# A conv, mixture-of-experts and Mamba-style block on one core: the second expert product with its weights stationary, and the image added during dispatch

## The chip, the cores and the metric

The kernel runs on one core of a Trainium2 chip. The time is the device time of one execution, in microseconds (us). A core has five engines that take their instructions in order, each from its own queue, and meet only through semaphores: TensorE (PE, the matmuls; its weight loads are shown apart as PEld), VectorE (DVE), ScalarE (ACT), GpSimd (POOL) and SyncE (SP, which here only issues DMA transfers). POOL also issues the indirect transfers, the scatters.

## The reference

The input x is 32 images of 128 channels by 56 x 56 points, float32; T = 32 x 3136 = 100352 tokens, C = 128. Two layers follow each other.

```python
# layer 0
x = depthwise_conv7x7(input) + dw_bias            # then NHWC
x = layernorm(x) * ln_gamma + ln_beta
logits = x.reshape(T, C) @ Wg + bg                # 8 experts
topv, topi = top_k(logits, 2); wts = softmax(topv)
# tokens in order of falling wts[:, 0]; an expert takes at most cap = 15680 rows
h = gelu(einsum('ecd,edf->ecf', eb, W1) + b1)     # 512 hidden channels
y = einsum('ecf,efd->ecd', h, W2) + b2
moe = sum over the two experts of y[slot] * gate
out0 = input + x + layer_scale * moe
# layer 1
xh = cv1 @ out0;  l = silu(batchnorm(dwconv3x3(xh)))
g = mamba(layernorm(xh))                          # a scan over 3136 points, 256 channels, 16 states
out = out0 + cv2 @ concat(l, g)
```

## The kernel before

The program has five stages, one after the other, with DRAM buffers between them.

*Convolution and layer norm* (lines 304 to 468). A depthwise convolution as banded matmuls, the norm, the router's logits. A normalized row is stored in `res_d`, one row of 128 floats for each token. Within two image rows (112 tokens, `TT`) the columns come out mirrored, so a row of `res_d` isn't in image order; `perm` is the 112 x 112 matrix that undoes this.

*Routing* (475 to 672). A counting loop finds for each expert the limit of its capacity, then every (token, choice) pair gets a slot: a row of `buf_d`, or a spare row behind the 8 x 15680 real ones where the expert is full. Beside it, 28 transfers write the real rows of `buf_d` with zeros and, in the last column, the token number T (lines 481 to 486). A row of `buf_d` has 130 words: 128 values, the gate, and the number of the row in `res_d` it goes back to.

*Dispatch* (834 to 865). 56 iterations. Each loads 14 x 128 rows of `res_d` into `xg` (line 853, six buffers), ACT copies them for the second choice (854), DVE writes the gates and the row numbers (856, 857; the numbers come from `backs`, made by an iota at 843), and POOL issues 28 scatters of 128 rows into `buf_d` (859). In the middle of it the weights of layer 1 are prepared.

*Experts* (871 to 957). For each of 8 experts, 31 groups of up to 512 rows (30 full ones and one of 320). A group is loaded as `xb` (945, ten buffers), transposed on PE into `ept` (951), copied by ACT to `xc` (953). `products` is called for the group before: four matmuls of 512 columns with a slice of W1 stationary and `xc` moving (890), each followed by a Gelu on ACT into `hh` (893); then for each of four tiles of 128 rows four matmuls with `hh` stationary and a slice of W2 moving (897), so that the result `py` has one row on one partition; DVE adds the bias (903), multiplies by the gate (906); POOL scatters 128 rows at a time and adds them to `res_d` (911), with a bounds check that leaves out rows with number T. In float32 each matmul is two instructions, a transpose is one. The order on each engine is made by a list scheduler from the program's order. The weights of an expert are loaded into one of two buffers (929 to 938): those of expert e + 2 as soon as expert e is done, and W2 and b2 are multiplied by the layer scale on DVE (935, 938).

*Layer 1* (960 to 1430). 224 groups of 448 points, 16 states each, in an order written out by hand (`PLAN`, `UNITS`): each step has a place in units of a state, and all are sorted by it. `fetch` (1011) loads 448 points of the input image (`x1`) and the rows of `res_d` (`yg`); `moe_pe` (1022) makes their sum in PSUM, with the image through the identity and the rows through `perm`, and `moe_act` (1032) copies it to `x1`, from which everything else follows. DVE scans the states (1373, 1377) and shares the products with POOL (1397); POOL makes `db` (1336), ACT the exponentials (1354), PE sums the products (1286).

Of the kernel before, what the change touches and what calls it, by code (L numbers as in the profile page):

```python
# [5 lines left out]
F32 = mybir.dt.float32  # L6
# [238 lines left out]
def tile_kernel(tc: tile.TileContext, a: dict, out: bass.AP):  # L245
# [14 lines left out]
    with (  # L260
# [6 lines left out]
        res_d = dram.tile([T, C], F32, name="res_d")  # L267

        ident = const.tile([128, 128], F32, name="ident")
        make_identity(nc, ident)  # L270
        mean_w = const.tile([128, 128], F32, name="mean_w")
# [203 lines left out]
        with (  # L475
# [5 lines left out]
            zero = rt.tile([128, ZT, RW], F32, name="zero")  # L481
            nc.gpsimd.memset(zero, 0.0)
            nc.gpsimd.memset(zero[:, :, C + 1].bitcast(I32), T)
            buf_t = buf_d[: E * CAP].rearrange("(p k) c -> p k c", p=128)
            for k in range(0, E * CAP // 128, ZT):
                nc.sync.dma_start(out=buf_t[:, k : k + ZT, :], in_=zero)
# [188 lines left out]
        def weights(wp, wt, pw):  # L675
# [86 lines left out]
            nc.tensor.matmul(p[:, 0:1], lhsT=mean_w, rhs=cv1b, start=True, stop=True)  # L762
# [71 lines left out]
        with (  # L834
# [3 lines left out]
            tc.tile_pool(name="disp", bufs=6, reuse_waits="tile") as dp,  # L838
        ):
            backs = []  # L840
            for k in range(2):
                bi = dc.tile([128, QB, TT], I32, name=f"bi{k}")
                nc.gpsimd.iota(bi, pattern=[[TT, QB], [1, TT]], base=0, channel_multiplier=PT)
                backs.append(bi)

            XT = 14
            res_b = res_d[:T, :].rearrange("(j q p) c -> q j p c", q=QB, p=TT)
            for q in range(QB):
                for p0 in range(0, TT, XT):
# [5 lines left out]
                    for k, xg in enumerate(xgs):  # L855
                        nc.vector.tensor_copy(xg[:, :, C], gates[k][:, o : o + XT])  # L856
                        nc.vector.tensor_copy(xg[:, :, C + 1].bitcast(I32), backs[k][:, q, ps])
                        for j in range(XT):
                            apart(nc.gpsimd.indirect_dma_start(  # L859
                                out=buf_d[:, :],  # L860
                                out_offset=bass.IndirectOffsetOnAxis(ap=slots[k][:, o + j : o + j + 1], axis=0),
                                in_=xg[:, j, :], in_offset=None,
                            ), "scatter")
                if q == QB // 2:
                    w3 = weights(w3p, w3t, p3t)
# [5 lines left out]
        with (  # L871
# [3 lines left out]
            tc.tile_pool(name="eph", bufs=3, space=PSUM) as eph,  # L875
            tc.tile_pool(name="epy", bufs=2, space=PSUM) as epy,
        ):
            lsr = ew.tile([128, C], F32, name="lsr", bufs=1)
            nc.sync.dma_start(
                out=lsr, in_=a["L0_conv_layer_scale"].rearrange("c a b -> (c a b)").partition_broadcast(128)  # L880
            )
            todo = []

            def products(e, tiles, xb, xc, w1t, w2t, b1t, b2t):

                rows = sum(tiles)
                hh = eb.tile([128, KF, GT * 128], F32, name="hh")
                for k in range(KF):
                    ph = eph.tile([128, GT * 128], F32, name="ph")
                    nc.tensor.matmul(  # L890
                        ph[:, :rows], lhsT=w1t[:, k * 128 : (k + 1) * 128], rhs=xc[:, :rows], start=True, stop=True
                    )
                    nc.scalar.activation(hh[:, k, :rows], ph[:, :rows], AF.Gelu, bias=b1t[:, k : k + 1])  # L893
                py = epy.tile([128, GT, C], F32, name="py")
                for j, n in enumerate(tiles):
                    for k in range(KF):
                        nc.tensor.matmul(  # L897
                            py[:n, j, :], lhsT=hh[:, k, j * 128 : j * 128 + n], rhs=w2t[:, k, :],
                            start=k == 0, stop=k == KF - 1,
                        )  # L900
                ys = eb.tile([128, GT, C], F32, name="ys", bufs=6)
                for j, m, n in wholes(tiles):
                    nc.vector.tensor_tensor(  # L903
                        ys[:n, j:m, :], py[:n, j:m, :], b2t[:n].unsqueeze(1).to_broadcast([n, m - j, C]), ALU.add
                    )
                    nc.vector.tensor_tensor(
                        ys[:n, j:m, :], ys[:n, j:m, :], xb[:n, j:m, C : C + 1].to_broadcast([n, m - j, C]), ALU.mult
                    )

                for j, n in enumerate(tiles):  # L910
                    apart(nc.gpsimd.indirect_dma_start(  # L911
                        out=res_d[:, :],
                        out_offset=bass.IndirectOffsetOnAxis(ap=xb[:n, j, C + 1 : C + 2].bitcast(I32), axis=0),
                        in_=ys[:n, j, :], in_offset=None, bounds_check=last, oob_is_err=False, compute_op=ALU.add,
                    ), f"back{e}")
# [11 lines left out]
            last = nc.gpsimd.to_reg(T - 1)  # L927
            for e in range(E):
# [7 lines left out]
                b2t = ew.tile([128, C], F32, name="b2t")  # L936
                nc.sync.dma_start(out=b2t, in_=a["L0_conv_b2"][e].partition_broadcast(128))
                nc.vector.tensor_tensor(b2t, b2t, lsr, ALU.mult)
                for i0 in range(0, CAP, GT * 128):
                    rows = min(GT * 128, CAP - i0)  # L940
                    tiles = [min(128, rows - j) for j in range(0, rows, 128)]
                    xb = eb.tile([128, GT, RW], F32, name="xb", bufs=10)
                    for j, m, n in wholes(tiles):
                        r0 = e * CAP + i0 + j * 128
                        nc.sync.dma_start(
                            out=xb[:n, j:m, :],
                            in_=buf_d[r0 : r0 + (m - j) * n, :].rearrange("(k p) c -> p k c", p=n),
                        )
                    pt = ept.tile([C, GT * 128], F32, name="ept")
                    for j, n in enumerate(tiles):  # L950
                        nc.tensor.transpose(pt[:, j * 128 : j * 128 + n], xb[:n, j, :C], ident[:n, :n])  # L951
                    xc = eb.tile([C, GT * 128], F32, name="xc")
                    nc.scalar.copy(xc[:, :rows], pt[:, :rows])
                    if todo:
                        products(*todo.pop())
                    todo.append((e, tiles, xb, xc, w1t, w2t, b1t, b2t))
            products(*todo.pop())


# [9 lines left out]
def layer1(s):  # L969
# [5 lines left out]
    mm_tile, res_d, x_d, out_d = s["mm_tile"], s["res_d"], s["x_d"], s["out_d"]  # L975
    perm = s["perm"]
# [5 lines left out]
    with (  # L982
# [28 lines left out]
        def fetch(g):  # L1011
# [3 lines left out]
            d["x1"] = three.tile([C, CH1], F32, name="x1", bufs=5)  # L1015
            nc.sync.dma_start(out=d["x1"], in_=x_d[n, :, q * CH1 : (q + 1) * CH1])
            d["yg"] = two.tile([TT, TPC1, C], F32, name="yg")
            nc.sync.dma_start(
                out=d["yg"], in_=res_d[t0 : t0 + CH1, :].rearrange("(j p) c -> p j c", p=TT)
            )  # L1020

        def moe_pe(g):
# [3 lines left out]
            nc.tensor.matmul(p[:, :CH1], lhsT=ident, rhs=d["x1"], start=True, stop=False)  # L1026
            for j in range(TPC1):
                nc.tensor.matmul(
# [3 lines left out]
        def moe_act(g):  # L1032
            d = st[g]
            nc.scalar.copy(d["x1"], d.pop("p_moe")[:, :CH1])
# [431 lines left out]
```

## Time and profile before

| | us |
|---|---|
| median of 14 runs | 15843.06 (15838.17 to 15858.88) |
| the profiled execution | 15853.05 |
| its span, first to last instruction | 15851.3 |
| convolution and norm, up to the last store of `res_d` | 0 to 1535 |
| routing, up to the first load of the dispatch | 1773 |
| dispatch, first scatter to last | 1779 to 3944 |
| experts, first load of `xb` to last scatter | 3946 to 5886 |
| layer 1, from the first load of `yg` | 5888 to 15851 |

All lines of a profile are in microseconds, unless marked ns. A line of the groups gives the line of the program, the engine, the operation, the tile written and the tiles read, the shapes, how often it ran, then the busy time and the mean of one in ns, then the idle time of the engine just before such instructions and what ended most of it. A line of the timeline gives the start, the duration, the engine, the line, the operation, the tiles, the shapes and the count, and in brackets the idle time before it and its releaser. "issue" means that nothing the profile shows was waited for. Matmuls overlap in their pipeline, so a matmul's own duration is longer than the distance to the next one. The two groups of scatters and the largest of layer 1 are:

```profile
L1336 POOL TENSOR_TENSOR db<-du,bb 128x1792 f32<-128x1792 f32 x1792 | 6579.1, 3683 | 0.1
L1373 DVE TENSOR_TENSOR_SCAN da<-da,db 128x898 f32<-128x898 f32 x2240 | 4521.8, 2019 | 0.6 <-issue 0.5
L859 POOL DMA_INDIRECT buf_d<-xg,slot x1568 | 1643.7, 1048 | 525.5 <-issue 521.0
L911 POOL DMA_INDIRECT res_d<-ys,xb x984 | 1592.6, 1619 | 349.2 <-issue 282.7
```

### The profile page before, as it was taken

What the parts mean: (1) busy time and instruction counts of PE and PEld (TensorE: products, weight loads), DVE (VectorE), ACT (ScalarE), POOL (GpSimd) and SP (SyncE); (2) the same over time, 40 slices, a digit from 0 to 9 for tenths busy, and PEclk for the clock granted to TensorE, in tenths of its full rate; (3) what the DMA queues carried; (4) which work ended last, traced back from release to release, by engine and by line L of the source; (5) the groups of instructions that cost most, each with busy time, mean ns of one, the idle gap of its engine ahead of it and who ended that gap; (6) DMA issues with size and microseconds to landing.
All of it is one profiled execution on the core that took longest, in us unless ns stands there. A gap on an engine that the chain in (4) does not pass through costs nothing. (4 is left out here: it accounts for less than half of the span.)

```text
span 15851.3 us, 247520 instructions
## 1 busy us (share of the span) xinstructions
PE 12825.1 (81%) x92981; PEld 7168.3 (45%) x92981; DVE 11114.2 (70%) x11366; ACT 10495.6 (66%) x21038; POOL 13327.5 (84%) x6330
## 2 busy tenths in 40 slices
PE   7996200000999999999999999999999999999998
PEld 7996100000777764444444444444444444444444
DVE  2655400000111119999999999999999999999999
ACT  4564300000444448888888888888888888888888
POOL 2343377777888879999999999999999999999999
PEclk9997555555999999999999999999999999999999
DMA  8785422222555545555555555555555555555555
GB/s 262 230 235 172 178 72 71 71 71 62 70 72 70 72 64 184 184 184 185 184 184 184 185 185 183 184 183 184 184 185 184 184 184 185 185 184 184 183 184 170
DMA packets 1325280, 2520.85 MB, mean 159 GB/s; under 512 B 139352, under 2 KB 777136, under 8 KB 1316400
## 3 DMA queue, kind: packets, MB, share of 16 engines
q1 hardware_dynamic: 1127600, 2310.57, 45.5%
q0 software_dynamic: 196480, 194.45, 7.0%
q8 instruction: 732, 11.99, 0.3%
q14 instruction: 468, 3.83, 0.1%
HBM read 2129.06 MB, written 375.43 MB: 158 GB/s over the span
## 5 line engine op out<-in xcount | busy, mean ns | idle before, releaser
L1336 POOL TENSOR_TENSOR db<-du,bb 128x1792 f32<-128x1792 f32 x1792 | 6579.1, 3683 | 0.1
L1354 ACT ACTIVATE da<-dt,aneg 128x449 f32<-128x449 f32 x7168 | 4540.2, 637 | 375.8 <-DVE r L1095 112.9
L1373 DVE TENSOR_TENSOR_SCAN da<-da,db 128x898 f32<-128x898 f32 x2240 | 4521.8, 2019 | 0.6 <-issue 0.5
L1286 PE MATMUL py<-prod,ident 64*64 64x448 f32 x28672 | 3225.9, 547 | 120.3 <-DVE prod L1397 112.8
L1397 POOL TENSOR_TENSOR prod<-hs,cb 128x896 f32<-128x896 f32 x1344 | 2605.0, 1938 | 219.4 <-issue 160.6
L1397 DVE TENSOR_TENSOR prod<-da,cb 128x896 f32<-128x896 f32 x2240 | 2439.0, 1089 | 132.4 <-DMA cb<-bc_d 17.1
L859 POOL DMA_INDIRECT buf_d<-xg,slot x1568 | 1643.7, 1048 | 525.5 <-issue 521.0
L911 POOL DMA_INDIRECT res_d<-ys,xb x984 | 1592.6, 1619 | 349.2 <-issue 282.7
L951 PE MATMUL ept<-ident,xb 128*128 128x128 f32 (+1 forms) x984 | 189.0, 274 | 2078.8 <-DMA xb<-buf_d 2078.2
L1373 DVE TENSOR_TENSOR_SCAN hs<-da,db 128x898 f32<-128x898 f32 x896 | 1785.2, 2013 | 0.1
L1286 PEld LDWEIGHTS py<-prod,ident 64*64 64x64 f32 x28672 | 1007.6, 132 | 1558.9 <-issue 1068.9
L1126 PE MATMUL p_xm<-te,wk 128*128 128x448 f32 x3584 | 1395.5, 540 | 0.0
L903 DVE TENSOR_TENSOR ys<-py,b2t 128x512 f32<-128x512 f32 (+2 forms) x256 | 170.8, 670 | 1729.5 <-PE py L897 1618.0
L856 DVE COPY xg<-gate 128x14 f32<-128x14 f32 x112 | 20.4, 185 | 1883.9 <-DMA buf_d<-xg,slot 1847.7
L854 ACT COPY xg<-xg 128x1792 f32<-128x1792 f32 x56 | 94.5, 1688 | 1821.5 <-DMA buf_d<-xg,slot 1773.2
L951 PEld LDWEIGHTS ept<-ident,xb 128*128 128x128 f32 (+1 forms) x984 | 124.6, 143 | 2082.5 <-issue 2081.3
L897 PEld LDWEIGHTS py<-w2t,hh 128*128 128x128 f32 x7872 | 938.0, 191 | 191.6 <-issue 119.4
L897 PE MATMUL py<-w2t,hh 128*128 128x128 f32 x7872 | 987.5, 279 | 14.8 <-ACT hh L893 9.4
L1126 PEld LDWEIGHTS p_xm<-te,wk 128*128 128x128 f32 x3584 | 671.6, 189 | 665.3 <-issue 567.5
L379 PE MATMUL pc<-xc,toep 112*112 112x112 f32 (+1 forms) x8192 | 939.1, 270 | 36.5 <-ACT toep L368 32.5
L1377 DVE TENSOR_TENSOR_SCAN hs<-da,db 128x449 f32<-128x449 f32 x896 | 925.0, 1075 | 0.5 <-ACT da L1354 0.3
L1258 PE MATMUL p_l<-xh,dwd 64*64 64x224 f32 x16128 | 907.1, 352 | 21.9 <-ACT dt L1240 2.2
(241 smaller groups left out, 20279.9 us busy)
## 6 DMA issues: line engine op xcount, KB each, us to landing
bb<-bc_d SPq DMA_DIRECT2D x1792, 448.0 KB
cb<-bc_d SPq DMA_DIRECT2D x1792, 448.0 KB
toep<-toep_d SPq DMA_DIRECT2D x448, 392.0 KB
buf_d<-zero SPq DMA_DIRECT2D x28, 2275.0 KB
xb<-buf_d SPq DMA_DIRECT2D x240, 260.0 KB
xt<-in_x SPq DMA_DIRECT2D x32, 1568.0 KB
res_d<-xa SPq DMA_DIRECT2D x128, 392.0 KB
xg<-res_d SPq DMA_DIRECT2D x56, 896.0 KB
```

The source lines that it names most:

```text
L379: nc.tensor.matmul(pc[:, c, :, lo:hi], lhsT=tp[c // 2][:, c % 2, 6 - 2 * o : 8 - 2 * o, :], rhs=s4[:, c, :, lo + o - 1 : hi + o - 1], star ...
L859: apart(nc.gpsimd.indirect_dma_start(out=buf_d[:, :], out_offset=bass.IndirectOffsetOnAxis(ap=slots[k][:, o + j : o + j + 1], axis=0), in_ ...
L897: nc.tensor.matmul(py[:n, j, :], lhsT=hh[:, k, j * 128 : j * 128 + n], rhs=w2t[:, k, :], start=k == 0, stop=k == KF - 1,)
L911: apart(nc.gpsimd.indirect_dma_start(out=res_d[:, :], out_offset=bass.IndirectOffsetOnAxis(ap=xb[:n, j, C + 1 : C + 2].bitcast(I32), axis= ...
L1126: nc.tensor.matmul(p[:, :CH1], lhsT=s["wk"][:, k, hs], rhs=d["te"][:, k : k + CH1], start=k == 0, stop=k == DC - 1 and not first,)
L1258: nc.tensor.matmul(d["p_l"][r][k * HD : (k + 1) * HD, : CH1 // 2], lhsT=s["dwd"][rs, t, rs], rhs=d["xh"][rs, dy + k * R : dy + (k + 1) * R ...
L1286: nc.tensor.matmul(ps[r][h * HD : (h + 1) * HD, :CH1], lhsT=lhsT(rs, h), rhs=rhs[rs, h, :], start=start, stop=stop,)
L1336: nc.gpsimd.tensor_tensor(dbp[i // 2].rearrange("p k (h t) -> p k h t", h=2)[:, :, :, 1:], st[g]["du"].unsqueeze(1).to_broadcast(both), un ...
L1354: e = nc.scalar.activation(da[:, h * W1 : (h + 1) * W1], st[g]["dt"][:, h, :], AF.Exp, scale=s["aneg"][:, h, i : i + 1])
L1373: scans.append(nc.vector.tensor_tensor_scan(hs, da, dbs[i], 0.0, ALU.mult, ALU.add))
L1377: scans.append(nc.vector.tensor_tensor_scan(hs2[h][:, hh], da[:, hh], dbs[i][:, hh], 0.0, ALU.mult, ALU.add))
L1397: eng.tensor_tensor(w["prod"], w["hs"][0][:, :, 1:], w["cb"], ALU.mult)
```

## The change

Five things change together.

1. A second row buffer `sum_d` takes the place of `res_d` as the target of the experts' scatters and the source of layer 1. It has T rows and 7 x 4480 spare rows.
2. In routing the empty rows of `buf_d` get the numbers of spare rows, different ones within an expert, in place of T: two zero tiles in turn, seven iotas, the same 28 transfers, and seven more that clear the spare rows of `sum_d`. The experts' scatters have no bounds check any more.
3. In dispatch 64 parts (`skip`) are added, two in each of the first eight iterations and one in each later one. A part loads half an image and its rows of `res_d`, adds them on PE (rows through `perm`, the image through the identity, both in row layout), ACT copies the sum, and a transfer stores it in `sum_d`. Since rows of `sum_d` are in image order, the iota of `backs` is mirrored within each image row.
4. In the experts W2 is stationary and `hh` moves: four matmuls of 512 columns, so that `py` has one channel on one partition. DVE adds the bias of that channel (`yt`), PE transposes back (`pb`), DVE multiplies by the gate. The copy to `xc` moves from ACT to DVE. A group passes through three steps in three turns of the loop: `enter`; `hidden` and `result`, the four products of one group in turn with those of the group before; `leave`. `eph` has two buffers in place of three, `epb` two.
5. In layer 1 `fetch` loads only the rows (of `sum_d`), and `moe_pe` is four transposes. `mean_w` has one column in place of 128.

```diff
+        VF = 7
+        sum_d = dram.tile([T + VF * FILL, C], F32, name="sum_d")
...
+            for v in range(VF):
+                zero = zeros[v % 2]
+                nc.gpsimd.iota(
+                    zero[:, :, C + 1].bitcast(I32), pattern=[[1, ZT]], base=T + v * FILL, channel_multiplier=ZT
+                )
+                for b in range(v, E * CAP // FILL, VF):
+                    nc.sync.dma_start(out=buf_t[b], in_=zero)
+            for v in range(VF):
+                nc.sync.dma_start(
+                    out=sum_d[T + v * FILL : T + (v + 1) * FILL].rearrange("(p k) c -> p k c", k=ZT),
+                    in_=zeros[v % 2][:, :, :C],
+                )
...
+            def skip(n, h):
+                t0 = (n * TPI + h * HT) * TT
+                xt = sk.tile([C, HT * TT], F32, name="xs")
+                nc.sync.dma_start(out=xt, in_=x_d[n, :, h * HT * TT : (h + 1) * HT * TT])
+                xr = sk.tile([TT, HT, C], F32, name="xr")
+                rows = [v[t0 : t0 + HT * TT, :].rearrange("(k p) c -> p k c", p=TT) for v in (res_d, sum_d)]
+                nc.sync.dma_start(out=xr, in_=rows[0])
+                for j0 in range(0, HT, 4):
+                    w = min(4, HT - j0)
+                    p = psk.tile([TT, 4, C], F32, name="p_sk")
+                    nc.tensor.matmul(p[:, :w], lhsT=perm, rhs=xr[:, j0 : j0 + w], start=True, stop=False)
+                    for j in range(w):
+                        nc.tensor.matmul(
+                            p[:, j, :], lhsT=xt[:, (j0 + j) * TT : (j0 + j + 1) * TT], rhs=ident,
+                            start=False, stop=j == w - 1,
+                        )
+                    nc.scalar.copy(xr[:, j0 : j0 + w], p[:, :w])
+                nc.sync.dma_start(out=rows[1], in_=xr)
...
+                    for _ in range(-(-len(parts) // (TT // XT * (QB - q) - p0 // XT))):
+                        skip(*parts.pop(0))
...
-                for j, n in enumerate(tiles):
-                    for k in range(KF):
-                        nc.tensor.matmul(
-                            py[:n, j, :], lhsT=hh[:, k, j * 128 : j * 128 + n], rhs=w2t[:, k, :],
-                            start=k == 0, stop=k == KF - 1,
-                        )
...
+            def enter(w, e, i0):
...
+                    nc.tensor.transpose(pt[:, j * 128 : j * 128 + n], xb[:n, j, :C], ident[:n, :n])
+                d["xc"] = eb.tile([C, GT * 128], F32, name="xc")
+                nc.vector.tensor_copy(d["xc"][:, :rows], pt[:, :rows])
...
+            def result(d, k):
...
+                nc.tensor.matmul(
+                    d["py"][:, :rows], lhsT=w2t[:, k, :], rhs=d["hh"][:, k, :rows], start=k == 0, stop=k == KF - 1
+                )
+                if k == KF - 1:
+                    d["yt"] = eb.tile([C, GT * 128], F32, name="yt")
+                    nc.vector.tensor_scalar(d["yt"][:, :rows], d["py"][:, :rows], b2t, None, ALU.add)
+
+            def leave(d):
+                tiles, xb = d["tiles"], d["xb"]
+                pb = epb.tile([128, GT, C], F32, name="pb")
+                for j, n in enumerate(tiles):
+                    nc.tensor.transpose(pb[:n, j, :], d["yt"][:, j * 128 : j * 128 + n], ident)
+                ys = eb.tile([128, GT, C], F32, name="ys", bufs=6)
+                for j, m, n in wholes(tiles):
+                    nc.vector.tensor_tensor(
+                        ys[:n, j:m, :], pb[:n, j:m, :], xb[:n, j:m, C : C + 1].to_broadcast([n, m - j, C]), ALU.mult
+                    )
+                for j, n in enumerate(tiles):
+                    apart(nc.gpsimd.indirect_dma_start(
+                        out=sum_d[:, :],
+                        out_offset=bass.IndirectOffsetOnAxis(ap=xb[:n, j, C + 1 : C + 2].bitcast(I32), axis=0),
+                        in_=ys[:n, j, :], in_offset=None, compute_op=ALU.add,
+                    ), f"back{d['e']}")
...
-                b2t = ew.tile([128, C], F32, name="b2t")
-                nc.sync.dma_start(out=b2t, in_=a["L0_conv_b2"][e].partition_broadcast(128))
-                nc.vector.tensor_tensor(b2t, b2t, lsr, ALU.mult)
+                b2t = ew.tile([C, 1], F32, name="b2t")
+                nc.sync.dma_start(out=b2t, in_=a["L0_conv_b2"][e].unsqueeze(1))
+                nc.vector.tensor_tensor(b2t, b2t, lsc, ALU.mult)
...
+            held = [None] * 3
+            for at in line + [None] * 3:
+                new = None
+                if at:
+                    if at[1] == 0:
+                        w = load_weights(at[0])
+                    new = enter(w, *at)
+                one, two, three = held
+                for k in range(KF):
+                    if one:
+                        hidden(one, k)
+                    if two:
+                        result(two, k)
+                if three:
+                    leave(three)
+                held = [new, one, two]
...
-            nc.tensor.matmul(p[:, :CH1], lhsT=ident, rhs=d["x1"], start=True, stop=False)
             for j in range(TPC1):
-                nc.tensor.matmul(
-                    p[:, j * TT : (j + 1) * TT], lhsT=yg[:, j, :], rhs=perm, start=False, stop=j == TPC1 - 1
-                )
+                nc.tensor.transpose(p[:, j * TT : (j + 1) * TT], yg[:, j, :], ident[:TT, :TT])
```

## The prediction

> **What bounds the kernel now.** I read the busy tenths first, to find the stages, then the busy time stage by stage, then one group of experts in the order of time, then the idle times by releaser.
>
> ```profile
> PE   7996200000999999999999999999999999999998
> DVE  2655400000111119999999999999999999999999
> POOL 2343377777888879999999999999999999999999
> ```
>
> A slice is 396 us. Convolution and routing fill four slices and a half, the dispatch lasts to slice 9, the experts to slice 14, layer 1 the rest. The table by stretches gives who is full in the dispatch, the experts and layer 1 (columns: stretch, length, busy us and instructions of PE, PEld, DVE, ACT, POOL, granted clock, DMA share, GB/s):
>
> ```profile
> 2400.00:3965.00 1565.00, 7.74 (x25) 4.47 (x25) 19.23 (x138) 61.90 (x40) 1173.44 (x1105) 0.50 0.23 69
> 4300.00:5700.00 1400.00, 1399.78 (x7999) 1011.54 (x7998) 255.71 (x389) 604.51 (x915) 1168.05 (x723) 1.00 0.52 71
> 6000.00:15851.00 9851.00, 9409.08 (x69459) 4409.65 (x69458) 9700.77 (x7563) 8540.69 (x17711) 9444.20 (x3401) 1.00 0.56 184
> ```
>
> The dispatch is POOL alone: POOL's idle is the 0.30 us between two scatters. Layer 1 is DVE: 98.5% busy, and of its waits only 17.1 us in 32 cases have a cause outside DVE worth naming (loads of cb). In the experts both PE and POOL look full, so one group must be read in order:
>
> ```profile
> 4804.53 0.36 PEld L951 LDWEIGHTS ept<-ident,xb 128*128 128x128 f32 x3
> 4804.97 3.60 PE L890 MATMUL ph<-xc,w1t 128*128 128x512 f32 x8
> 4805.56 0.69 DVE L906 TENSOR_TENSOR ys<-ys,xb 128x512 f32<-128x512 f32 x1
> 4805.84 1.84 POOL L911 DMA_INDIRECT res_d<-ys,xb  x1 [0.30 <-issue]
> 4807.99 1.55 POOL L911 DMA_INDIRECT res_d<-ys,xb  x1 [0.30 <-DMA res_d<-ys,xb]
> 4808.40 0.83 PE L897 MATMUL py<-w2t,hh 128*128 128x128 f32 x6
> 4809.34 2.98 PEld L897 LDWEIGHTS py<-w2t,hh 128*128 128x128 f32 x26 [0.24 <-ACT hh L893]
> 4812.68 3.60 PE L890 MATMUL ph<-xc,w1t 128*128 128x512 f32 x8
> ```
>
> From the first L890 to the next is 7.71 us (4812.68 - 4804.97). PE's part: eight L890 take 3.43 (to 4808.40), 0.429 each; 26 L897 go from 4801.63 to 4804.53 in the group before, 0.1115 each, so 32 take 3.57; three transposes (L951) go from 4804.53 to 4804.86, 0.11 each, four take 0.44; and a wait of 0.27 for the last Gelu. 3.43 + 3.57 + 0.44 + 0.27 = 7.71. PE sets the pace. POOL needs 4 x 1.855 = 7.42, plus the 0.29 of the scatter that meets L906, and runs some 11 us behind: the group whose L903 starts at 5862.0 is scattered from 5873.8.
>
> **The experts, part by part.** Each product is two instructions. *PE.* The second product becomes 8 instructions of 512 columns, the shape of L890: 8 x 0.429 = 3.43 in place of 3.57. Four transposes back (yt to pb) are added: 4 x 0.11 = 0.44. The wait of 0.27 goes, since the second product takes hh of the group before. New group: 6.86 + 0.88 = 7.74, that is +0.03, +7 us over 240 full groups; in the eight groups of 320 rows 24 short instructions (2.68) become 8 x 0.28 with three transposes (0.33), -1. Sum +6. Bounds: a transpose back between 0.107 (0.429/4, its columns alone) and 0.14 (mean weight load of L951): -3 to +30.
>
> [...] L951's single duration here is 274 ns, but three pass in 0.33; by 275 ns each the added four would cost 1.10 a group and the sum would be some 160 us worse. I go by the spacing in the row.
>
> *POOL.* Where the check goes, the nearest unchecked scatter is L859: 0.97 in its first 228 and about 1.10 later, without the addition. So between 1.40 and 1.855 each, 5.6 to 7.42 a group, below 7.74 on both ends: worth nothing on the path except at the end. Cover gone, it would set the pace above 1.935 each.
>
> *DVE* gets the xc copy that ACT did (0.59) and keeps two operations near 0.69: 2 us of 7.74. ACT keeps four Gelus, 2.75. The order matters more than the load. Of six experts, two waits stand in DVE's queue:
>
> ```profile
> 4450.57 0.69 DVE L935 TENSOR_TENSOR w2t<-w2t,lsr 128x512 f32<-128x512 f32 x1 [5.43 <-DMA w2t<-in_L_conv_W]
> 4456.50 0.29 DVE L938 TENSOR_TENSOR b2t<-b2t,lsr 128x128 f32<-128x128 f32 x1 [5.24 <-DMA b2t<-in_L_conv_b]
> ```
>
> DVE is held 5.43 + 0.69 + 5.24 + 0.29 = 11.65 us. Before, only L903 is queued behind, and POOL's backlog covers it (POOL idles once, 2.36). Now xc is behind it, and PE needs xc one group later: 11.65 + 0.59 - 7.74 = 4.5 late, six times, 27 us. If b2t (now 512 bytes) comes with w2t, nothing: 0 to +27, I take the middle, +13.
>
> *Start and end.* The first group waits some 18 us in its Gelus (3.51, 4.91 and 8.45 with releaser "remote"); kept, bounds -18 to 0. At the end PE's last L897 is at 5866.4 and the first yg load at 5887.9, 21.5 later, ten scatters of backlog. Now: yt, transposes and product about 2.4, seven scatters at 1.40 to 1.855 (9.8 to 13), 1.5 to land: 13.7 to 16.9. I take -8 (bounds -8 to -4).
>
> **Routing.** A second memset (3.89) before the first fill; seven iotas of 35 columns, each below the 0.76 of the 784-column one. From the third on an iota waits for the four transfers two fills back; behind it on POOL stand the mask and own_i, which are needed only after the counting loop, and POOL is idle 227 us. Fill: 28 transfers, 63.7 MB, keep the DMA full to about 1700; the seven of sum_d add 16 MB, at the 242 GB/s of the first xg loads (7 x 917 KB in 26.55) 66 us, to about 1770; the first xg load is issued at 1773. Cost 0, bounds 0 to +15; uncovered, 66.
>
> **Dispatch.** Each of 64 parts issues on SP two loads and a store of 803 KB (154 MB, 71 GB/s more on 69), on PE at the granted 0.50 seven-halves of 512 columns and 14 products of 128 (about 12 us, 780 in all of 2165), on ACT four copies (2.2). POOL issues none of it. Traffic as such doesn't slow a scatter: beside the first loads it took 0.97. The store waits for ACT's copies; behind it on SP stand the next xg loads, and POOL waits for these. A part is a chain of some 20 us (two loads of 3.2, 12, 2.2, a store), an iteration of 28 scatters 35.6 to 39; the first eight iterations hold two parts, 40 us, but xg is loaded five to six iterations ahead (the load at 1833.7 follows scatter 42). Cost 0, bounds 0 to +30.
>
> **Layer 1.** Per group the image product (2 x 0.39) and half of the eight short ones leave PE, about 1.1 us x 224, and a load of 229 KB leaves SP. Hidden under DVE: worth nothing, except for the waits on cb. -17 to +10; I take -9, half of them. The new x1 buffer is taken at the copy, later than now.
>
> **Sum.** +6 + 13 - 8 - 9 = +2. The profiled execution took 15853.05 (span 15851.3), 10 above the median 15843.06; the differences carry over. Forecast 15843 + 2 = **15845 us**.
>
> **Rivals.**
> *POOL takes over (slower).* The check was free, a scatter stays 1.855, and each of three DVE operations lengthens one by 0.29: 7.42 + 0.87 = 8.29, 0.55 above PE, x 246 = +135: **15980**. It decides above 1.935 a scatter. For it: POOL already needs all of 7.71. Against: L859's 1.27 to 1.40; chance 0.08.
>
> [...]
>
> *PE still waits in each group (slower).* If the transposes back or the first product of a group follow their DVE operation too closely, a wait like the 0.27 stays: x 246 = +66, **15911**; it decides from 0.13 a group (32 us). Against: every input is a group old. 0.12.
>
> *Dispatch late (slower).* SP runs the parts in order and lags 8 x 4 = 32 us: **15877**, more if later iterations lag too. For it: SP is one queue; against: five iterations of lead. 0.10.
>
> *The loose ends all go (faster).* No hold at the six experts, no start wait, no wait for cb: +6 - 8 - 18 - 17 = -37: **15806**. For it: these are all the waits the trace shows off the pace-setters; against: nothing in the change touches the 18. 0.22.
>
> **Numbers.** Forecast 0.48. A measurement here tells about 0.2%, 32 us, from no change: faster 0.22, same 0.48, slower 0.30. The range reaches to 15795 (start and cb waits gone) and to 15912 (one wait a group), leaving out the POOL rival and half of the waiting one. The forecast's own range is 15815 to 15875.
>
> **What would show it.** Right: PE's period near 7.74 with gapless L-lines for hidden and result; POOL idle between scatters, each 1.1 to 1.55; a held DVE at six places with a PE gap of about 4; dispatch from first to last scatter within 2165 + 30; layer 1 9965 within 10. Wrong: a period of 8 or more; scatters at 1.55 or above without gaps; POOL waiting for xg in the dispatch; transposes faster or slower than 0.11.

## The result, and the profile after

The changed kernel takes 16033.12 us (median of 6 runs, 16007.82 to 16040.88), the kernel before beside it 15844.87 (28 runs): 1.0117 times as long, 95% interval 1.0107 to 1.0126. It is 188 us slower, where 2 more were forecast. The profiled execution's span is 16022.6, 171.3 more than before's 15851.3. By stages:

| us | before | after | difference |
|---|---|---|---|
| first scatter of the dispatch at | 1779.0 | 1768.0 | -11.0 |
| dispatch, first scatter to last | 2164.5 | 2325.7 | +161.2 |
| last scatter to first load of `xb` | 2.4 | 2.2 | -0.2 |
| experts, first load of `xb` to first of `yg` | 1942.0 | 1927.9 | -14.1 |
| layer 1 | 9963.4 | 9998.8 | +35.4 |

The busy tenths of the changed kernel, and PEclk, the share of full speed that TensorE's clock was granted, in tenths, in 40 slices:

```profile
PE   7996223322799998999999999999999999999998
DVE  2655300000122228999999999999999999999999
POOL 2443466666788888999999999999999999999999
PEclk9997556655899999999999999999999999999999
```

In the dispatch (slices 4 to 9) POOL fell from 7 tenths to 6: the engine that is alone there now waits. The same stretches as before's, of the changed kernel (length, busy us and instructions of PE, PEld, DVE, ACT, POOL, granted clock, DMA share, GB/s):

```profile
2400.00:4090.00 1690.00, 502.90 (x1867) 339.36 (x1865) 27.91 (x186) 172.92 (x255) 1087.91 (x1137) 0.59 0.48 140
4300.00:5700.00 1400.00, 1400.00 (x4372) 705.60 (x4371) 356.45 (x567) 498.62 (x731) 1129.62 (x726) 1.00 0.53 71
6100.00:16022.00 9922.00, 9223.74 (x68392) 4235.76 (x68384) 9740.95 (x7592) 8567.53 (x17768) 9480.50 (x3413) 0.99 0.54 178
```

PE is now wholly full in the experts, and in layer 1 its granted clock is 0.99, not 1.00. The two groups of scatters:

```profile
L991 POOL DMA_INDIRECT sum_d<-ys,xb x984 | 1532.5, 1557 | 395.2 <-issue 253.5 <-DVE ys L987 137.2 <-DVE xc L954 3.5
L902 POOL DMA_INDIRECT buf_d<-xg,slot x1568 | 1502.3, 958 | 824.7 <-issue 478.7 <-DMA xg<-res_d 173.7 <-ACT xg L897 125.3
```

A scatter of the dispatch became shorter (958 ns against 1048), and outside POOL's waits scatters stay 1.26 us apart, where before they slowed to 1.40. That 1.40 is a mean, here as in the prediction: before, 1219 of 1567 distances are below 1.35 us and 119 are 2 us or more. But POOL now waits for `xg`, for its load (173.7) or ACT's copy (125.3). Before it never did. Distances over 3 us between scatters: 28, together 381 us; before, one. What holds `xg` is seen in ACT's timeline of the changed kernel (start, duration, line, tiles; in brackets the idle time before, "remote" where the profile doesn't tell what ended it):

```profile
1787.10 0.59 ACT L886 COPY xr<-p_sk 112x512 f32<-112x512 f32 x1 [8.19 <-issue]
1787.58 1.69 ACT L897 COPY xg<-xg 128x1792 f32<-128x1792 f32 x1
1809.52 0.59 ACT L886 COPY xr<-p_sk 112x512 f32<-112x512 f32 x1 [20.26 <-issue]
1836.12 0.59 ACT L886 COPY xr<-p_sk 112x512 f32<-112x512 f32 x1 [26.02 <-issue]
1852.93 0.37 ACT L886 COPY xr<-p_sk 112x256 f32<-112x256 f32 x1 [16.22 <-remote]
```

and in PE's, of the same part:

```profile
1780.45 1.02 PE L880 MATMUL p_sk<-xr,perm 112*112 112x512 f32 x2
1781.31 1.04 PE L882 MATMUL p_sk<-ident,xs 128*112 128x128 f32 x8
1787.73 1.20 PE L880 MATMUL p_sk<-xr,perm 112*112 112x256 f32 x2 [5.39 <-issue]
1788.72 1.06 PE L882 MATMUL p_sk<-ident,xs 128*112 128x128 f32 x4
```

These are the third piece of the part (four times 112 tokens) and its last (twice 112). By the records their products end at 1782.4 and 1789.8; ACT's copies, which wait for nothing but them, run at 1836.12 and 1852.93: 54 and 63 us late. The trace keeps no semaphore update of PE between 1777.87 and 1852.90. The next ones are at 1880.90, 1908.90, 1936.20 and 1953.70, each 0.02 to 0.07 us before one of ACT's copies, for products whose records end at 1866.92, 1869.70, 1871.43 and 1883.66. So what comes late is the products' completion, the semaphore update that tells ACT of it. Successive copies are 22.4, 26.6 and 16.8 us apart: 32, 38 and 24 steps of 0.70. A whole piece has 20 PE instructions (ten matmuls, ten weight loads), the last has 12: up to two steps, 1.40 us, for each (the next whole pieces come 28.0 us apart, 40 steps). Of 256 such copies 157 start more than 2 us after their products' end; before 108 of them ACT sat idle for more than 2 us after its own last work was done too.

### The profile page after: what moved, and what is told of

Same layout as the page of the kernel before. It is cut to its first block, busy times and chain, and to the rows that moved or that the text cites. A ratio compares the mean times of both kernels' runs of the same rounds, so it can differ in the third digit from the quotient of the medians.

```text
span 16022.6 us, 239944 instructions
## 1 busy us (share of the span) xinstructions
PE 13225.5 (83%) x89037; PEld 6981.6 (44%) x89037; DVE 11255.1 (70%) x11607; ACT 10477.0 (65%) x21046; POOL 13133.1 (82%) x6337
## 5 line engine op out<-in xcount | busy, mean ns | idle before, releaser
L902 POOL DMA_INDIRECT buf_d<-xg,slot x1568 | 1502.3, 958 | 824.7 <-issue 478.7
L991 POOL DMA_INDIRECT sum_d<-ys,xb x984 | 1532.5, 1557 | 395.2 <-issue 253.5
L880 PE MATMUL p_sk<-xr,perm 112*112 112x512 f32 (+1 forms) x512 | 364.4, 805 | 1563.1 <-issue 921.9
L966 ACT ACTIVATE hh<-ph,b1t 128x512 f32<-128x512 f32 (+1 forms) x992 | 676.7, 682 | 1277.3 <-PE ph L963 1269.2
L886 ACT COPY xr<-p_sk 112x512 f32<-112x512 f32 (+1 forms) x256 | 132.4, 535 | 1962.1 <-remote 1404.4
L978 DVE TENSOR_SCALAR yt<-py,b2t 128x512 f32<-128x512 f32 (+1 forms) x248 | 184.4, 744 | 1371.4 <-PE py L973 1356.6
L963 PE MATMUL ph<-xc,w1t 128*128 128x512 f32 (+1 forms) x1984 | 1005.8, 589 | 0.0
L973 PE MATMUL py<-hh,w2t 128*128 128x512 f32 (+1 forms) x1984 | 1002.4, 587 | 0.0
```

The source lines that it names most:

```text
L902: apart(nc.gpsimd.indirect_dma_start(out=buf_d[:, :], out_offset=bass.IndirectOffsetOnAxis(ap=slots[k][:, o + j : o + j + 1], axis=0), in_ ...
L963: nc.tensor.matmul(ph[:, :rows], lhsT=w1t[:, k * 128 : (k + 1) * 128], rhs=d["xc"][:, :rows], start=True, stop=True)
L973: nc.tensor.matmul(d["py"][:, :rows], lhsT=w2t[:, k, :], rhs=d["hh"][:, k, :rows], start=k == 0, stop=k == KF - 1)
L991: apart(nc.gpsimd.indirect_dma_start(out=sum_d[:, :], out_offset=bass.IndirectOffsetOnAxis(ap=xb[:n, j, C + 1 : C + 2].bitcast(I32), axis= ...
```

## The experiments

Two kinds of chip turned up (by the record's numbers, chip 12 and chips 3, 7 and 13). Beside `image_back`, `pe_filled`, `rows_only` and `parts_filled` the kernel before took 15657 us, and its scatters (seen in `image_back`, whose dispatch is that of the kernel before) stay 1.27 apart to the end, dispatch 1992. In all other runs it took 15852 or 15853, near the 15845 of the result: 1.40 apart in the mean, dispatch 2165. Each run is to be read against the kernel before beside it.

| run | us | kernel before | dispatch | experts | layer 1 |
|---|---|---|---|---|---|
| image_back | 15657.62 | 15657.06 | 1992.0 | 1927.5 | 9964.0 |
| pe_filled | 16181.29 | 15657.06 | 1996.9 | 2447.0 | 9962.7 |
| rows_only | 15682.60 | 15657.06 | 1979.5 | 1928.0 | 9999.2 |
| parts_filled | 16134.07 | 15657.06 | 1978.8 | 1932.5 | 10001.6 |
| changed_again | 16013.20 | 15853.23 | 2331.8 | 1927.5 | 10002.1 |
| before_again | 15855.35 | 15853.23 | 2165.4 | 1940.7 | 9968.8 |
| l1_filled | 15968.96 | 15853.23 | 2281.8 | 1927.7 | 9965.0 |
| image_back_b | 15853.24 | 15852.07 | 2164.9 | 1946.5 | 9965.9 |
| rows_only_b | 15892.47 | 15852.07 | 2167.4 | 1946.6 | 10000.7 |
| pe_paced | 16172.26 | 15852.07 | 2367.2 | 2056.7 | 9964.5 |
| own_queue | 16107.64 | 15852.07 | 2377.6 | 1935.5 | 10000.0 |
| repaired | 15913.08 | 15852.63 | 2220.6 | 1942.9 | 9966.4 |
| scatters_spaced | 15981.01 | 15852.63 | 2273.4 | 1927.8 | 10001.6 |

**image_back and image_back_b: the experts alone.** From the changed kernel, the parts are taken out, the experts scatter into `res_d`, layer 1 is that of before.

```diff
-                    for _ in range(-(-len(parts) // (TT // XT * (QB - q) - p0 // XT))):
-                        skip(*parts.pop(0))
...
-                        out=sum_d[:, :],
+                        out=res_d[:, :],
...
+            nc.tensor.matmul(p[:, :CH1], lhsT=ident, rhs=d["x1"], start=True, stop=False)
```

> The new experts alone: the image is added in layer 1 as before, dispatch and layer 1 are those of before, the experts scatter into res_d with spare rows. Theory: nothing of the changed kernel's loss is in the experts; dispatch back to 2165 us, layer 1 back to 9963. If the experts keep their gain of 14, about 15820 us. Rival: that gain was the 18 us of first Gelus with a late PE, which fell away only because PE had worked during the dispatch; then the wait is back and the kernel takes about 15840, no faster than before.

> The new experts alone once more (image added in layer 1, dispatch and layer 1 of before), wanted beside a kernel before of 15850 us, where the scatters come 1.40 us apart. Theory A: the experts' gain is the 18 us wait of the first Gelus, which goes with PE work in the dispatch; here PE is idle in the dispatch, the wait stays, experts 1942, whole 0 to +5 against before. Theory B: the pipeline itself gains 14, experts 1928, whole 14 to 25 less than before. Beside a kernel before of 15657: as in image_back, same as before.

Ratios 1.000, intervals 0.999 to 1.001 and 0.999 to 1.0009. Dispatch and layer 1 are back, so both losses belong to the image's move. Beside the 15852 theory A holds: the start of the experts is late again.

**rows_only and rows_only_b: fewer PE instructions in a part.**

```diff
-                    for j in range(w):
-                        nc.tensor.matmul(
-                            p[:, j, :], lhsT=xt[:, (j0 + j) * TT : (j0 + j + 1) * TT], rhs=ident,
-                            start=False, stop=j == w - 1,
-                        )
```

> The changed kernel without the image's products in the parts (the image is left out of the result): a part has 16 instructions of PE in place of 72, the same transfers, copies and order on SP. Theory (what a part waits for is PE's completions, some 1.40 us for each matmul and weight load while scatters run): a part takes at most 22 us, less than an iteration, POOL no longer starves, dispatch about 2000 and the whole about 15710 us. Rival (the order on SP and the 154 MB of transfers hold xg, whatever PE does): dispatch stays at 2326 within 30, the whole at 16033 within 30.

> The parts without the image's products (left out of the result), 16 PE instructions a part in place of 72, wanted beside a kernel before of 15850 us, where the changed kernel has 29 gaps of POOL in the dispatch, 387 us in all. Theory (each PE instruction of a part is completed some 1.40 us apart there): a part takes 22 us, POOL has no gap, dispatch 1980 to 2010, the whole some 320 us below the changed kernel, 15690 to 15720. Rival (order on SP and traffic): gaps as before, dispatch 2280 to 2330, the whole 15970 to 16030.

With the same transfers, copies and order on SP, POOL has no gap left in either run. For the chip with 15657 that tells nothing, since there `parts_filled`, with all the products, has no gap either. On the chip with 15852 the lag itself shrank with the count (ACT's timeline of `rows_only_b`):

```profile
1872.52 0.58 ACT L881 COPY xr<-p_sk 112x512 f32<-112x512 f32 x1 [3.86 <-PE p_sk L880]
1877.42 0.37 ACT L881 COPY xr<-p_sk 112x256 f32<-112x256 f32 x1 [4.32 <-remote]
1883.02 0.58 ACT L881 COPY xr<-p_sk 112x512 f32<-112x512 f32 x1 [5.23 <-remote]
```

Pieces of 4 PE instructions come 4.9 to 5.6 us apart, 1.2 to 1.4 an instruction. The expected 1980 to 2010 was missed there: without gaps the scatters fall to 1.40 as in the kernel before, and the dispatch is 2167.

**pe_filled, parts_filled and pe_paced: is it PE's half clock?** Idle matmuls whose result nobody reads: in the kernel before, behind each part of the changed one, and, paced by `xg`, in `image_back` (the edit shown).

```diff
+                    for j in range(30):
+                        nc.tensor.matmul(
+                            p_fill.rearrange("p (a c) -> p a c", c=C), lhsT=ident,
+                            rhs=xgs[1][:, 3 * (j % 4) : 3 * (j % 4) + 4, :C], start=True, stop=True,
+                        )
```

> The kernel before with 36 idle matmuls of 512 columns (zeros, never read) on PE in each iteration of the dispatch, 56 x 36 x 0.86 = 1734 us of PE work. Theory: with PE idle for long the scatters come 1.40 us apart and the first experts' products are signalled late; with PE at work the pace stays at 1.27: dispatch 1568 x 1.265 = 1985 in place of 2165, start of the experts 18 less, about 15650 us. Rival (the pace falls because of the scatters' own queue): dispatch 2165, at most the 18 gone, 15825 to 15845.

> The changed kernel with 18 idle matmuls of 512 columns on PE behind each part (64 x 18 x 0.86 = 991 us of PE work). Theory (the completions are late because PE falls to half clock between parts): the lag of the copies goes, dispatch 2000 to 2050, the whole about 15720 us. Rival (they are late because of the number of PE instructions beside scatters): 36 more instructions a part, at 1.40 each 50 us a part: dispatch over 3000 us; or no effect, 16033.

> image_back with 30 idle matmuls of 512 columns on PE in each iteration of the dispatch, reading that iteration's xg copy, so that PE works 26 of each 36 us to the end; the weights of layer 1 are prepared after the third iteration. Theory (with an idle PE the completions of the whole core come in steps of 0.70 us, so that scatters are 1.40 apart and the first experts' products late): beside a kernel before of 15850, scatters 1.27 apart to the end, dispatch 1992, experts 1928, the whole 15650 to 15680, 180 us faster than before. Rival (the scatters' pace has nothing to do with PE): dispatch 2165, the whole as image_back. Second rival (PE instructions beside scatters are what is slow): 60 more of them an iteration at 1.40 each, dispatch over 4000.

The first two ran where the scatters stay at 1.27 anyway, so they don't tell about the half clock; there the idle work ran on past the dispatch (the first `xb` is transposed late in `pe_filled`, loaded 450 us late in `parts_filled`), which makes them slow. `parts_filled` tells something else: on that chip, with 72 instructions a part and the idle ones behind them, no copy of the 256 starts more than 0.1 us after both its products' end and ACT's last work, POOL has no gap and the dispatch takes 1978.8. The completions are on time there.

`pe_paced` ran beside 15852. PE was granted 0.60 to 0.81 in the dispatch. POOL's line of it:

```profile
L876 POOL DMA_INDIRECT buf_d<-xg,slot x1568 | 1518.2, 968 | 850.4 <-issue 474.7 <-ACT xg L871 369.3 <-DMA buf_d<-xg,slot 6.1
```

There are no parts in this kernel, yet POOL waits 369 us for ACT's copy of `xg`, which waits for PE to be done with the buffer (1066 us in 25 waits): 30 gaps, 410 us. Between the gaps the scatters are 1.27 apart, as the theory said, but so they are between the gaps of the changed kernel, so the pace doesn't speak for the clock. More PE work beside the scatters made gaps here; it didn't remove them. And completions are late at full clock too. PE's line, then ACT's:

```profile
2081.57 1.22 PE L832 MATMUL p_wo<-cvgt,wop 128*128 128x128 f32 x4 [5.88 <-issue]
```

```profile
2096.65 0.37 ACT L836 COPY wo<-p_wo 128x256 f32<-128x256 f32 x1 [10.94 <-remote]
```

The copy starts 13.9 us after its product ends (2082.79), and from 2085 to 2096 PE's granted clock was 1.00. The half clock as cause falls. The idle matmuls left at the end run for 139 us more, so the experts' first product is 130 us late and the experts take 2056.7.

**changed_again and before_again: the repeat.**

> The changed kernel itself, beside the kernel before. In the runs of image_back the kernel before took 15657 us, not 15845, and the scatters of the dispatch came 1.27 us apart to the end, not 1.40. Theory: PE's completions in the parts are late only where the scatters also run at 1.40 in the kernel before; where the kernel before takes 15657, the changed one has a dispatch near 1985 and takes about 15657 + 35 of layer 1 - 7 = 15685. Rival: the parts starve POOL everywhere: 1.0117 times the kernel before, 15840 where it takes 15657.

> The kernel before, profiled in the same place as the changed one. Theory: where the pace of the scatters stays at 1.27 to the end (dispatch 1992), the experts' first products are signalled without the 18 us wait too, and the experts take 1924 to 1930 in place of 1942. Rival: the 18 us are there in any case, 1942.

1.01 (1.0083 to 1.0117): the loss is there again, with 29 gaps of 387 us. The 18 us at the start of the experts are there again too (1940.7). What the changed kernel alone does where the kernel before takes 15657 wasn't measured; the nearest is `parts_filled`, which has the same parts and no gap there, as the theory has it.

**own_queue: the order on the queues.**

```diff
-                nc.sync.dma_start(out=xr, in_=rows[0])
+                nc.scalar.dma_start(out=xr, in_=rows[0])
...
-                    nc.scalar.copy(xgs[1][:, :, :C], xgs[0][:, :, :C])
+                    nc.vector.tensor_copy(xgs[1][:, :, :C], xgs[0][:, :, :C])
```

> The changed kernel with the parts' loads and stores issued by ACT in place of SP, and the copy of xg for the second choice on DVE in place of ACT, so that neither the loads nor the copies of xg stand behind a part. Theory: POOL no longer starves and the dispatch's scatters take 1985, but the parts still get their completions late; beside a kernel before of 15850 a part takes some 100 us while scatters run, 20 are done when they end, and the other 44 follow at 12 to 17 us each before the experts' first scatter can land: the whole 16200 to 16450. Rival (only the order on the queues was bad, PE's completions are on time when POOL doesn't stop): parts done with the dispatch, the whole 15690 to 15720.

Both were wrong: POOL still starves, 17 gaps of 385 us, the whole 16108. The waits of SP's queue in the dispatch say why:

```profile
SPq L896 <- DMA xr<-res_d: 547.2, 9, 134.6
SPq L896 <- DMA xs<-in_x: 446.6, 8, 103.0
SPq L896 <- DMA sum_d<-xr: 277.6, 5, 92.6
```

The load of `xg` (L896) waits for the parts' transfers, 1271 us in 22 waits, though ACT issues those and SP's queue is left to it. In the changed kernel's trace the 5607 transfers that SP issues complete on eight semaphores; that the load shares these with the parts' transfers here too is read from the waits. Copies of the parts stay up to 81 us late. The path through which a late part reaches POOL changed; the lateness did not.

**repaired: a part of 44 PE instructions.** The image is turned by transposes into a second PSUM tile that DVE adds; with the matmul of `l1_filled`.

```diff
-                        nc.tensor.matmul(
-                            p[:, j, :], lhsT=xt[:, (j0 + j) * TT : (j0 + j + 1) * TT], rhs=ident,
-                            start=False, stop=j == w - 1,
-                        )
+                        nc.tensor.transpose(pt[:, j, :], xt[:, (j0 + j) * TT : (j0 + j + 1) * TT], ident)
...
+                    nc.vector.tensor_tensor(xr[:, j0 : j0 + w], xr[:, j0 : j0 + w], pt[:, :w], ALU.add)
```

> The changed kernel with the image turned in the parts by transposes (one instruction and one weight load for 112 tokens in place of two and two) into a second PSUM tile that DVE adds, 44 PE instructions a part in place of 72; and the matmul of l1_filled in layer 1. Beside a kernel before of 15850 us. Theory: at 1.40 us for each PE instruction a part takes some 60 us while scatters run, so 2165/60 = 36 of the 64 parts pass beside the scatters; the rest pass in POOL's gaps, which shrink from 387 us to 50 to 170; dispatch 2150 to 2210, layer 1 9964, start and experts as in the changed kernel; the whole 15820 to 15880. Rival (gaps don't go with the number of PE instructions, but come from the order on SP): dispatch 2280 to 2330, the whole 15950 to 16000.

Gaps 257 us, dispatch 2220.6, the whole 15913.08 (1.0043, 1.0029 to 1.0056): between the two ends, but more than the 50 to 170 expected, and no version that beats the kernel before. The late start of the experts is back as well (1942.9). So beside 15852, with 16, 44 and 72 instructions a part, the gaps are 0, 257 and 338 to 387 us (three profiles, with `l1_filled`).

**scatters_spaced: slower scatters.**

```diff
+                            nc.gpsimd.memset(pad, 0.0)
```

> The changed kernel with a POOL memset of 128x128 after each scatter of the dispatch (not the first 28), so that scatters come 1.6 to 2.0 us apart in place of 1.26. Beside a kernel before of 15850. Theory A (PE's completions are late only because scatters are issued faster than the 1.40 us at which they come in the kernel before): copies follow their products within 1 us, POOL's gaps for xg nearly gone (under 50 us), dispatch 1568 x the new spacing, 2500 to 3100. Theory B (scatters at any pace make each PE instruction take 1.40): lags of 27 us a chunk and gaps of 200 us or more stay on top of it.

The memset took 0.22 us and fell mostly into POOL's 0.30 between scatters: 1.35 apart, not 1.6 to 2.0. That was enough to tell: whole pieces that ACT waits more than 2 us for come 11.3 us after the copy before them in the median, 23.6 in `changed_again` by the same count, and gaps are 141 us against 338 to 387. The dispatch is 2273, against 2326 and 2332 in the changed kernel, but `l1_filled`, with the same dispatch as the changed kernel, has 2282; so slower scatters cost nothing here, and a gain isn't shown. Neither theory had the size right; A's direction holds.

**l1_filled: the work that left PE in layer 1.**

```diff
+            nc.tensor.matmul(
+                p[:, :CH1], lhsT=ident[:TT, :], rhs=yg.rearrange("p j c -> p (j c)")[:, :CH1], start=True, stop=True
+            )
```

> The changed kernel with one more matmul of 448 columns per group in moe_pe (the rows through the identity, overwritten by the transposes), in the place where the image product stood: 0.8 us of PE work. Theory (the work taken from PE lets it pause in each fifth group long enough to fall to half clock for 3.4 us, which makes p_z and after it ACT and DVE late): no half-clock windows, layer 1 back from 9999 to 9963, 35 us faster than the changed kernel run beside it. Rival (layer 1 is slower for another reason: the later x1 buffer, the traffic of sum_d): 9999, same time as the changed kernel.

Layer 1 is 9965.0 against 10002.1 beside it: 37 us gained by a useless matmul, of 44 in the medians. `repaired`, with the same matmul, has 9966.4. (The dispatch, untouched, is 50 shorter in this profile: gaps of 338 us, not 387. It varies.) The mechanism can be read in the changed kernel. PE first, then ACT:

```profile
7088.95 0.60 PE L1093 MATMUL p_moe<-ident,yg 112*128 112x112 f32 x4
7091.23 1.77 PE L1350 MATMUL py<-prod,ident 64*64 64x448 f32 x8 [1.68 <-DVE prod L1461]
7092.93 2.63 PE L1202 MATMUL p_z<-te,wz 128*128 128x448 f32 x4
```

```profile
7092.65 0.53 ACT L1098 COPY x<-p_moe 128x448 f32<-128x448 f32 x1
7094.83 0.63 ACT L1210 ACTIVATE zs<-p_z,zb 128x448 f32<-128x448 f32 x1 [1.65 <-PE p_z L1202]
```

The transposes end early, PE pauses 1.68 us for DVE's product, and its granted clock is 0.5 for the next 3.41 us: eight short products take 1.77 us where eight took 0.98 at 7088.04. So `p_z` is late, ACT waits 1.65, and behind ACT the carries that DVE needs. DVE's waits from 7024 to 15024, changed kernel, and from 7000 to 15000, `l1_filled`:

```profile
DVE hs L1441 <- ACT db L1469: 18.5, 27, 0.7
DVE prod L1461 <- ACT db L1469: 8.0, 33, 0.3
DVE da L1437 <- issue: 6.9, 12, 1.0
DVE prod L1461 <- DMA cb<-bc_d: 6.0, 12, 0.9
```

```profile
DVE prod L1464 <- DMA cb<-bc_d: 13.4, 24, 1.3
```

## Why the prediction was wrong

The period that PE sets in the experts was right; the two places that were called hidden were not, and the rest of the experts' sum came out near by terms that miss both ways.

*Dispatch, "Cost 0, bounds 0 to +30": +161. This is the step that failed.* It rests on "A part is a chain of some 20 us (two loads of 3.2, 12, 2.2, a store)". The 12 us of PE are what its instructions take one after the other (L880 and L882 were busy 697 us for 64 parts, 11 each); until their completions arrive 98 us pass (three pieces of 27, one of 17) when scatters run. The lead of "five to six iterations" lasts 158 us: the first gap begins at 1926. The gaps cost 381 - 28 x 1.26 = 346 us, and scatters 1.263 apart give 2164.5 - 1567 x 1.263 = 185 back: +161. The rival "Dispatch late" had the path right (store behind ACT's copies, `xg` behind the store) and priced it 32, from work and not from completions. The kernel before had shown the thing: its first Gelus, of which the prediction said "kept" and "nothing in the change touches the 18". ACT's timeline of before:

```profile
3958.59 0.69 ACT L893 ACTIVATE hh<-ph,b1t 128x512 f32<-128x512 f32 x1 [3.51 <-remote]
3964.19 0.69 ACT L893 ACTIVATE hh<-ph,b1t 128x512 f32<-128x512 f32 x1 [4.91 <-remote]
3973.33 0.69 ACT L893 ACTIVATE hh<-ph,b1t 128x512 f32<-128x512 f32 x1 [8.45 <-remote]
```

The waits are 5, 7 and 12 steps of 0.70, right after 1568 scatters, for products that PE's own records end at 3954.2, 3955.0 and 3956.3. That was the price list for PE work beside scatters. A scatter itself settles at two such steps there: the last 100 of the kernel before come 1.400 us apart in the mean.

*Layer 1, "Hidden under DVE: worth nothing", -9 with bounds -17 to +10: +35.* The waits for `cb` did halve (12.6 to 6.0 us in 8000; before's from 6888 to 14888), as hoped. But PE does not run at one speed. From 100 us after the first load of layer 1 to 300 us before its end, the granted clock fell to 0.5 in 47 windows of 3.41 us after, in none before and none in `l1_filled`.

There one pause of 1.67 to 1.94 us in each group, 216 in all, came with half clock 47 times; before and in `l1_filled`, with no pause above 1.45 us, half clock never came. `l1_filled` adds work and shortens the pause at once, so which of the two the clock answers to isn't told apart.

*Experts.* From the first load to the fourth group's first product: 47.1 to 26.0, -21 where 0 was taken and -18 was the bound. That is the 18 us wait, and losing it was luck, not a gain of the new experts: it is back in `image_back_b` (44.6). Near 15850 it goes with the time that scatters had run since POOL's last long gap: 88 to 90 us in the changed kernel's profiles and `l1_filled` (25.6 to 26.0), 178 in `own_queue` (33.6), 229 in `repaired` (40.9), no long gap at all in `image_back_b` and before; only `scatters_spaced`, 1.35 apart, has none after 586 (25.8). From the fourth group to the last: 1865.3 to 1871.5, +6, the +6 of the PE term; the period is 7.74 as worked out. The hold of DVE, +13 (0 to +27), did not come: no later group takes over 7.85. It was the prediction's own case for 0: `b2t` no longer waits behind `w2t` (0.15 us right after it), and DVE is held 7.3 us on average at six experts. End: +1, not -8: eleven scatters follow the last product where seven were counted, and an unchecked one takes 1.557 + 0.30 = 1.86, what the checked one took; the term's 1.40 to 1.855 had it at the upper end. Sum -14.

*"POOL takes over".* Its first condition came true, the check was free. Its second did not: a scatter is 1.557 on average beside three DVE operations a group, 4 x 1.86 = 7.43 stays under 7.74. *"PE still waits in each group"*: it does not, PE is 1400.00 of 1400 us busy.

*Routing, 0 to +15*: -11 to the first scatter (-3.5 in the repeat).

## What to carry to other kernels

Work put on an idle engine beside another engine's critical stream is priced by when its completions arrive (here 98 us for a part while scatters run), not by its busy time (here 11): look in the trace of before for any place where the two already run side by side, and read the waits there. Taking work from an engine that is not the bound can slow the kernel: here PE's longest pauses in layer 1 grew from 1.45 to 1.94 us, its granted clock fell to 0.5 in 47 windows, and the layer took 35 us more. A filler tells in one run.

## What the runs showed of the hardware

What makes the completions late is not settled. Shown is: where the kernel before takes 15845 to 15853, PE's instructions beside scatters 1.26 us apart complete up to 1.40 apart, and beside scatters 1.35 apart in about half of that (11.3 us a whole piece against 23.6); the lag falls within POOL's longer gaps (2364.5 to 2389.3 in the changed kernel: 63.1 us at 2367.8, 6.2 at 2378.4, none at 2381.9), though in the kernel before it lasts 30 us beyond the last scatter (3943.5 to 3973.3); it goes with the count of PE instructions (gaps of 0, 257 and 338 to 387 us with 16, 44 and 72 a part), and keeping PE busy didn't cure it (410 us of gaps in `pe_paced`).

One rival no run tests: the recording of the trace. In layer 1 the trace has 16 semaphore updates for each transfer, before (71664 for 4479) and after (68096 for 4256), and practically as many in every other run. Of 16 for each transfer in the dispatch it keeps all in the four runs beside 15657, but only 10 to 22% in every other run (3286 of 26416 before, 5459 of 29472 after). In the kernel before, most are missing from the first scatters to about 3980, just after the last late Gelu at 3973.33. So late completions and lost records go together. Every run that the record lists has a span and a granted clock, so it was recorded; whether recording delays the completions, or one cause lies behind both, a run without recording could tell. Until then the 161 us hold for recorded runs on such a chip.

On the chip where it takes 15657, the scatters keep 1.27 to the end, and the first Gelus of the experts aren't late. `image_back`, run on both, differs by 196 us, of which 173 lie in the dispatch and 19 in the experts; why the chips differ is open too.
